# The y sums of a selective scan move into the side work's PSUM bank, and the side work is grouped anew

## The chip, the cores and the metric

The kernel runs on one core of a Trainium2 chip. The metric is the time of one execution on the device in microseconds; before the change the median of three runs is 2876.79 us (2875.39 to 2877.91). All data are float32.

## The reference, cut to what matters

One layer for x of shape [2, 1024, 512]: a gated state-space scan with a residual and a layer norm, then a gated feed-forward block with a residual and a layer norm.

```python
xn = x * rsqrt(mean(x * x) + 1e-6) * norm_w
xn = xn * sigmoid((xn @ select_proj_w.T + select_proj_b) * select_gate)
delta, B_ssm, C_ssm = split(xn @ x_proj_w.T)            # 128 columns each
delta = softplus(delta @ dt_proj_w.T + dt_proj_b)       # [.., 512]
A = -exp(A_log)                                         # [512, 128]
def step(h, inp):                                       # once for each token
    dt, bt, ct, xt = inp
    h = exp(dt[:, :, None] * A) * h + (dt * xt)[:, :, None] * bt[:, None, :]
    y = einsum('bdn,bn->bd', h, ct)
    return h, y
x = layernorm(x + (y + x * D_param) @ out_proj_w.T)
x = layernorm(x + (silu(x @ w_gate.T) * (x @ w_up.T)) @ w_down.T)   # hidden 2048
```

The state h has 512 x 128 values for each batch entry.

## The kernel before

**The scan.** The 2048 tokens are cut into 64 states of S = 32 tokens. The 128 partitions hold the n of the state. A state has two halves, and a half holds 256 of the 512 d's; it is worked in eight steps (r = 0 to 7), each with 32 d's of 32 tokens. So there are 64 x 2 x 8 = 1024 steps k, and the loop over k writes the order of every engine's instructions out by hand.

A step has these instructions, in this order. TensorE makes a group of four matmuls: for b = 0 and 1, `bu` (u times B, L692) for this step, and `a` (A times dt, `decay_mm`, L404) for the next step. ScalarE takes the exponential of each `a` into SBUF (`decay_exp`, L411). VectorE adds what the state before carries over to the first column of each run of tokens (L705) and runs one scan of 1024 elements (L708), which writes a slice of `hs[h]`. The four matmuls of a group stand in four different row strips of the array and run at the same time. GpSimd makes the operands of the groups (`diag`: `ddt` L375, `du` L385).

**C h.** `y_round(h, b)` (L423) sums C h over the partitions for four tokens of a half: four matmuls in four column strips. Eight rounds make a half. They are put into the steps of the next half by `ROUNDS`: rounds 0 to 2 at r = 1, 3 to 5 at r = 4, 6 and 7 at r = 7. Both halves of a state gather in one PSUM bank, `ps_y`. When a state is done, `y_out` copies the bank (ScalarE, L436) and picks and adds the wanted columns (GpSimd, L437 to L439), at r = 0 of the second half of the next state.

**Side work.** What is not the scan is written as Python generators. `pre` makes a lot of 256 tokens ready (names ss, sel, xp, b, z, uT, t0). `post` ends a tile of 128 tokens (zT transposes, op the output projection, layer norm). `ffn` is the feed-forward block of a tile (x1T transposes; gu: gate and up, eight items of eight parts; d: down, four items of eight parts). A generator yields "P" before it takes the bank for an item of matmuls, "H" between the item's parts, and "E" where another engine goes on. Every item takes the one bank of `ps_m` (`misc`), so an item can start only when the item before has been read out: gu by a ScalarE copy (L547), sel and z by ScalarE activations, d by a VectorE add (L567), op and zT by VectorE adds (L474, L461).

**The planner.** `Work.others()` runs at the start of every step and moves each generator that stands at "E" on by one. `Work.tensor()` issues one part: of the item that holds the bank, or of the first generator that waits for it. `PARTS` gives a step its number of parts: up to 4, 3, 3, 3, 3 at r = 0, 2, 3, 5, 6; parts not used are kept as a credit of up to 6, of which a step takes 4 at most. One part is 0.43 to 0.5 us of TensorE: two matmuls of 128 columns (gu), or one of 256 (d, op, sel, xp). Steps with C h have no parts. A lot must be ready before its first state (`work.finish`). What is left of the side work at the loop's end runs in a tail.

**PSUM.** Eight banks: four for `bu` (two buffers of two), two for `a`, one for y, one for the side work.

Of the kernel before, what the change touches and what calls it, by code (L numbers as in the profile page):

```python
# [9 lines left out]
FP = mybir.dt.float32  # L10
AF = mybir.ActivationFunctionType
# [6 lines left out]
TC = 256  # L18


ROUNDS = ((), (0, 1, 2), (), (), (3, 4, 5), (), (), (6, 7))
PARTS = (4, 0, 3, 3, 0, 3, 3, 0)
RMS_EPS = 1e-6
LN_EPS = 1e-5

# [9 lines left out]
def kernel(  # L35
# [83 lines left out]
    pre_pool = tc.alloc_tile_pool(name="pre", bufs=1)  # L119
    step_pool = tc.alloc_tile_pool(name="step", bufs=2)  # L120
    half_pool = tc.alloc_tile_pool(name="half", bufs=2)
    ps_y = tc.alloc_tile_pool(name="ps_y", bufs=1, space=PSUM)
    ps_m = tc.alloc_tile_pool(name="ps_m", bufs=1, space=PSUM)

    bank_pool = [tc.alloc_tile_pool(name="ps_m0", bufs=6, space=PSUM)]
# [39 lines left out]
    def pre(c):  # L165
# [31 lines left out]
        yield "E"  # L197
        for m in range(NM):
            nc.scalar.activation(xT[:, m, :], xT[:, m, :], AF.Copy, scale=col(V_NORM, m))
        yield "P"  # L200
        ps = misc(f"ss_{c}")
        for k in range(NM):
            nc.tensor.matmul(  # L203
# [9 lines left out]
        for a in (slice(0, 2), slice(2, 4)):  # L213
# [1 line left out]
                xn[:, a, :], xT[:, a, :], rms.unsqueeze(1).to_broadcast([P, 2, n]), ALU.mult  # L215
            )
            yield "E"
        yield "P"


        for m in range(NM):
            ps = misc(f"sel_{c}_{m}")
            yield from matmuls(ps, sel_w, m, xn)
            nc.scalar.activation(
                u[:, m, :], ps[:, 0:n], AF.Relu,
                bias=neg[:, 1, m : m + 1], scale=neg[:, 0, m : m + 1],
            )
            nc.scalar.activation(
                dt[:, m, :], ps[:, 0:n], AF.Abs, bias=gate_b[:, m : m + 1], scale=col(V_GATE, m)
            )  # L230
            yield "P" if m + 1 < NM else "E"
        yield from softplus(dt, u)
        nc.scalar.activation(dt, dt, AF.Exp, scale=-1.0)
        yield "E"
        for a in (slice(0, 2), slice(2, 4)):
            nc.gpsimd.tensor_tensor(xn[:, a, :], xn[:, a, :], dt[:, a, :], ALU.mult)
            yield "E"
        yield "P"


        for g, dst in ((0, low), (2, c_sb)):
            ps = misc(f"xp_{c}_{g}")
            yield from matmuls(ps, xp_w, g, xn)
            nc.scalar.copy(dst, ps[:, 0:n])
            yield "P"

        ps = misc(f"b_{c}")
        for j in range(n_j):
# [8 lines left out]
        for st in range(n_s):  # L257
# [2 lines left out]
                ub_d[t0 // S + st, :, :, 1, :].rearrange("g t n -> t g n"),  # L260
                rows.unsqueeze(1).to_broadcast([S, 4, N]),
            )
        yield "P"

        for a in range(0, NM, 2):
            ps = misc(f"z_{c}_{a}")
            for m in (a, a + 1):
                nc.tensor.matmul(  # L268
                    ps[:, ts(m - a, n)], dt_w[:, ts(m, P)], low, start=True, stop=True
                )  # L270
                yield "H" if m == a else "E"
            for m in (a, a + 1):
                z = ps[:, ts(m - a, n)]
                nc.scalar.activation(u[:, m, :], z, AF.Relu, bias=col(V_DTB, m))
                nc.scalar.activation(dt[:, m, :], z, AF.Abs, bias=col(V_DTB, m))
            yield "P" if a == 0 else "E"
        yield from softplus(dt, u)
        for a in (slice(0, 2), slice(2, 4)):
            nc.gpsimd.tensor_tensor(u[:, a, :], dt[:, a, :], xn[:, a, :], ALU.mult)
            yield "E"  # L280

        for j in range(n_j):
            yield "P"
            ps = misc(f"uT_{c}_{j}")
            for m in range(NM):
                nc.tensor.transpose(ps[:, ts(m, P)], u[:, m, ts(j, P)], ident)
                if m == 1:
                    yield "H"
            yield "E"
            t = pre_pool.tile([P, D], FP, tag="row", name=f"uT_{c}_{j}")  # L290
            nc.scalar.copy(
                t.rearrange("p (g m c) -> p m g c", g=4, m=NM),
                ps.rearrange("p (m g c) -> p m g c", m=NM, g=4),
            )
            for st in range(4):
                nc.sync.dma_start(
                    ub_d[t0 // S + 4 * j + st, :, :, 0, :].rearrange("g t q -> t g q"),
                    t[ts(st, S), :].rearrange("t (g q) -> t g q", g=4),
                )
            if c == 0:  # L300
                load(0)
                diag(0, 0)
                diag(0, 1)
        yield "P"
        ps = misc(f"t0_{c}")
        for m in range(NM):
            nc.tensor.matmul(
# [40 lines left out]
    def carry_a(st):  # L348

        if st % NSB == 0:  # L350
            return
        cd = carried[st]
        nc.gpsimd.tensor_tensor(cd, a_n, cd, ALU.mult)
        nc.scalar.activation(cd, cd, AF.Exp, scale=-1.0)

    def carry_h(st, i):

# [57 lines left out]
    def y_round(h, b):  # L415


        st, i = divmod(h, 2)
        if i == 0 and b == 0:
            ys[st] = ps_y.tile([P, 512], FP, tag="y", name=f"y_{st}")  # L420
        at = 28 + 28 * b
        for m in range(NM):
            nc.tensor.matmul(  # L423
                ys[st][ts(m, 32), ts(i, 256)], cz[st % 3][:, at : at + 32],
                hs[h][:, ts(m, 64), ts(b, 4)],
                start=(i == 0 and b == 0), stop=(i == 1 and b == 7),
                skip_group_check=True,
            )

    def y_out(st):  # L430

        tt, s = divmod(st, 4)
        if s == 0:
            yrs[tt] = post_pool.tile([P, 4, P], FP, tag="yr", name=f"yr_{tt}")
        yc = post_pool.tile([P, P, 4], FP, tag="yc", name=f"yc_{st}")
        nc.scalar.copy(yc, ys.pop(st).rearrange("p (q t) -> p q t", t=4))  # L436
        nc.gpsimd.tensor_tensor(yc, yc, pick.unsqueeze(1).to_broadcast([P, P, 4]), ALU.mult)  # L437
        nc.gpsimd.tensor_tensor(yc[:, :, 0:2], yc[:, :, 0:2], yc[:, :, 2:4], ALU.add)
        nc.gpsimd.tensor_tensor(yrs[tt][:, s, :], yc[:, :, 0], yc[:, :, 1], ALU.add)  # L439
        if s == 3:  # L440
            work.add(post(tt), front=True)

    yrs = {}
# [1 line left out]
    def post(tt):  # L445
# [4 lines left out]
        yield "E"  # L450
        nc.gpsimd.tensor_tensor(zT, zT, dq.unsqueeze(2).to_broadcast([P, NM, P]), ALU.mult)
        yield "E"
        yield "P"
        ps = misc(f"zT_{tt}")
        for s in range(4):
            nc.tensor.transpose(ps[:, ts(s, P)], yrs[tt][:, s, :], ident)
# [6 lines left out]
        )  # L463
        x1 = post_pool.tile([P, D], FP, tag="x1", name=f"x1_{tt}", bufs=4)
        nc.sync.dma_start(x1, xf[tt])
        yield "P"
        ps = misc(f"op_{tt}")
        for half in (slice(0, 256), slice(256, 512)):
            for k in range(NM):
# [20 lines left out]
    def ffn(tt, row):  # L490
# [22 lines left out]
            yield "E"  # L513
        fetch(4)
        x1T = ffn_pool.tile([P, NM, P], FP, tag="x1T", name=f"x1T_{tt}")
        yield "P"
        ps = misc(f"x1T_{tt}")
        for m in range(NM):
            nc.tensor.transpose(ps[:, ts(m, P)], row[:, ts(m, P)], ident)
# [5 lines left out]
        for what in order:  # L525
            part = int(what[1])
            if what[0] == "g":
# [2 lines left out]

                for f in range(0, NH, 2):
                    fetch(at + 4)
                    yield "P"
                    ps = misc(f"gu_{tt}_{part}_{f}")
                    for b in range(2):
                        w = pieces[at + b].rearrange("p (a k h) -> p a k h", a=2, k=NM)
# [17 lines left out]
                yield "E"  # L554
            for half in range(2):
                fetch(at + 4)
                yield "P"
                ps = misc(f"d_{tt}_{part}_{half}")
                for f in range(NH):
                    w = pieces[at + f // 4].rearrange("p (f d) -> p f d", f=4)  # L560
                    nc.tensor.matmul(  # L561
                        ps[:, 0:HD], hid[:, f, :], w[:, f % 4, :],
                        start=(f == 0), stop=(f == NH - 1),
                    )
                    yield "H" if f + 1 < NH else "E"
                part_of = row[:, ts(half, HD)]
                nc.vector.tensor_tensor(part_of, part_of, ps[:, 0:HD], ALU.add)  # L567
                at += 2
# [38 lines left out]
    class Work:  # L607


        def __init__(self):  # L610
            self.gens, self.holder = [], None

        def add(self, gen, front=False):
            item = [gen, next(gen)]
# [13 lines left out]
                        self.holder = None  # L628
                    self.step(item)

        def tensor(self):

            if self.holder is not None:
                if self.holder[1] != "H":
                    return False
                self.step(self.holder)
                return True
            for item in self.gens:
                if item[1] == "P":
                    self.holder = item  # L640
                    self.step(item)
                    return True
            return False

        def finish(self, item):
            while item in self.gens:
# [13 lines left out]
    bank_pool.pop().release()  # L660
    bank_pool.append(ps_m)
    ps_bu = tc.alloc_tile_pool(name="ps_bu", bufs=2, space=PSUM)
    ps_a = tc.alloc_tile_pool(name="ps_a", bufs=2, space=PSUM)
    for b in range(2):
        decay_exp(0, b, decay_mm(0, b))

    pres, begun, credit = {}, set(), 0
    for k in range(NG):
        h, m, pair = place(k)
        st, i = divmod(h, 2)  # L670
        r = k % 8
        work.others()
        if r == 0:
            hs[h] = half_pool.tile([P, 256, S], FP, tag="h", name=f"h_{h}")

            if i == 1 and st:
                y_out(st - 1)
            if i == 0:
                c = lot_of[st]
                if c + 1 < NC and c not in begun:  # L680
                    begun.add(c)
                    pres[c + 1] = work.add(pre(c + 1), front=True)
                if st + 1 < NS:
                    if lot_of[st + 1] > c:
                        work.finish(pres[c + 1])
                    load(st + 1)
# [24 lines left out]
            bu.rearrange("p q t -> p (q t)"),  # L711
            0.0, ALU.mult, ALU.add,
        )
        if h:
            for b in ROUNDS[r]:
                y_round(h - 1, b)
        credit = min(credit + PARTS[r], 6)
        for _ in range(min(credit, 4) if PARTS[r] else 0):
            if not work.tensor():
                break  # L720
            credit -= 1

        j, r4 = divmod(k, 4)
        if r4 == 3:
# [7 lines left out]
                carry_h(st + 1, 0)  # L732
        if r == 5 and i == 0 and st + 1 < NS:
            carry_a(st + 1)
    for j in range(8):
        y_round(2 * NS - 1, j)
    y_out(NS - 1)
    ps_a.release()
    ps_bu.release()
    bank_pool[0] = tc.alloc_tile_pool(name="ps_m2", bufs=6, space=PSUM)  # L740
# [4 lines left out]
        work.others()  # L745
        work.tensor()

    for pool in (bank_pool[0], ps_m, ps_y, hid_pool[0], ffn_pool, post_pool, main):
        pool.release()


# [65 lines left out]
```

## Time and profile before

| | |
|---|---|
| median of 3 runs | 2876.79 us |
| the profiled execution | 2875.05 us, span 2873.2 us |
| mean granted TensorE clock | 0.985 |
| TensorE, VectorE busy | 2751.4 us (96%), 2532.2 us (88%) |
| GpSimd, ScalarE busy | 1783.0 us (62%), 1561.8 us (54%) |
| scans, L708 | 1024, 2287 ns each |
| exponentials, L411 | 2048, 585 ns each |
| DMA | 258.66 MB, mean 90 GB/s |

In the groups, a line gives the code line, engine, operation, tiles, shapes and count, then the busy time and the mean of one, then the idle time of the engine ahead of it and who ended it. An fp32 matmul leaves two records, so "x16" of gu is eight matmuls. The time from the first `bu` record of a step to that of the next is called a step's length here; the time from it to the first record of the run behind the group is 1.07 us where nothing waits. Busy time alone says little: the two busiest engines take turns in waiting for each other.

### The profile page before, as it was taken

The page shows a single profiled execution, that of the slowest core. Times are in us where ns is not written, and L with a number is a line of the kernel's source. Part 1 is how long each engine was busy: PE and PEld are TensorE (multiplying, and loading weights), DVE is VectorE, ACT ScalarE, POOL GpSimd, SP SyncE. Part 2 cuts the span into 40 slices and gives each one's busy share as a digit, 9 for nine tenths or more (in the row PEclk, how much of TensorE's full clock was granted, in tenths as well). Part 3 has the DMA queues.
Part 4 walks back from the last instruction along what each step waited for, and adds up shares of the span by engine and source line. Part 5 has one row for each costly group of instructions (what it writes and reads, how often), then busy time and mean ns, then how long its engine had stood idle before and what let it go on. Part 6 is the DMA issues. An engine that isn't in the chain of part 4 may idle for free.

```text
span 2873.2 us, 57382 instructions
## 1 busy us (share of the span) xinstructions
PE 2751.4 (96%) x22728; PEld 1496.3 (52%) x22728; DVE 2532.2 (88%) x2176; ACT 1561.8 (54%) x3105; POOL 1783.0 (62%) x2016
## 2 busy tenths in 40 slices
PE   7879899999999999999999999999999999999998
PEld 4324455555555555455555555555555555555558
DVE  3999799899998999999999999999999999999970
ACT  4545555555565556645555555555556555555543
POOL 4556665666666666666567667566665666666643
PEclk6999999999999999999999999999999999999999
DMA  2011221324213231222312233122321322333236
GB/s 74 16 30 65 78 87 61 105 66 133 85 53 112 89 107 62 82 98 89 111 51 88 97 103 109 56 84 92 114 96 51 115 96 91 114 101 100 98 112 230
DMA packets 112379, 258.66 MB, mean 90 GB/s; under 512 B 11568, under 2 KB 49456, under 8 KB 112112
## 3 DMA queue, kind: packets, MB, share of 16 engines
q1 hardware_dynamic: 112112, 254.99, 27.4%
q8 instruction: 181, 2.97, 0.4%
q14 instruction: 86, 0.70, 0.1%
HBM read 242.23 MB, written 12.71 MB: 89 GB/s over the span
## 4 chain that ended last, share of the span: by engine, by line
PE 75%; DVE 18%; issue 3%; ACT 2%; POOL 1%; DMA 0%; SPq 0%; DVEq 0%; POOLq 0%; ACTq 0%
PE bu L692 27%; PE gu L539 17%; DVE h L708 16%; PE y L423 13%; PE d L561 6%; PE a L404 5%; PE sel L186 2%; PE op L470 1%; PE xp L186 1%; DVE bu L705 1%; ACT a_sb L411 1%; PE b L250 1%; PE ss L203 0%; PE z L268 0%; DMA ub_d<-uT 0%
## 5 line engine op out<-in xcount | busy, mean ns | idle before, releaser
L708 DVE TENSOR_TENSOR_SCAN h<-a_sb,bu 128x1024 f32<-128x1024 f32 x1024 | 2341.2, 2287 | 160.7 <-PE bu L692 46.3
L411 ACT ACTIVATE a_sb<-a 128x496 f32<-128x496 f32 x2048 | 1089.0, 585 | 1078.5 <-PE a L404 957.1
L404 PE MATMUL a<-ddt,a_t 32*128 32x512 f32 x4096 | 1253.9, 647 | 3.0 <-ACT t L314 2.8
L692 PE MATMUL bu<-du,ub 32*128 32x512 f32 x4096 | 1210.5, 647 | 47.9 <-DVE h L708 27.3
L375 POOL TENSOR_TENSOR ddt<-dt,hot 128x512 f32<-128x512 f32 x512 | 532.6, 1048 | 310.2 <-PE a L404 310.2
L539 PEld LDWEIGHTS gu<-x1T,w 128*128 128x128 f32 x4096 | 482.2, 192 | 230.9 <-issue 181.3
L385 POOL TENSOR_TENSOR du<-ub,hot 128x512 f32<-128x512 f32 x512 | 535.0, 1049 | 48.9 <-PE a L404 44.9
L539 PE MATMUL gu<-x1T,w 128*128 128x128 f32 x4096 | 537.1, 283 | 11.7 <-DVE x L474 4.0
L692 PEld LDWEIGHTS bu<-du,ub 32*128 32x128 f32 x4096 | 342.9, 185 | 376.9 <-issue 206.8
L423 PE MATMUL y<-h,cz 128*32 128x256 f32 x8192 | 527.3, 386 | 1.3 <-DVE h L708 1.3
L423 PEld LDWEIGHTS y<-h,cz 128*32 128x32 f32 x8192 | 228.2, 110 | 407.8 <-issue 296.4
L404 PEld LDWEIGHTS a<-ddt,a_t 32*128 32x128 f32 x4096 | 379.4, 185 | 31.3 <-ACT a_sb L411 19.9
L579 POOL TENSOR_SCALAR gu<-gu 128x256 f32<-128x256 f32 x128 | 108.3, 846 | 309.6 <-ACT gu L547 309.3
L705 DVE TENSOR_TENSOR bu<-bu,cd 128x32 f32<-128x32 f32 x992 | 185.6, 187 | 98.2 <-PE a L404 92.0
L561 PE MATMUL d<-w,hid 128*128 128x256 f32 x1024 | 256.7, 393 | 12.6 <-ACT t L314 4.4
L561 PEld LDWEIGHTS d<-w,hid 128*128 128x128 f32 x1024 | 183.9, 190 | 131.7 <-issue 86.1
L437 POOL TENSOR_TENSOR yc<-yc,pick 128x512 f32<-128x512 f32 x64 | 66.5, 1039 | 151.1 <-ACT yc L436 151.0
L362 POOL TENSOR_TENSOR cd<-cd,h 128x256 f32<-128x256 f32 x124 | 106.4, 858 | 45.5 <-DVE h L708 45.5
L587 POOL TENSOR_TENSOR hid<-gu,e 128x256 f32<-128x256 f32 x128 | 93.0, 727 | 62.1 <-ACT e L585 60.2
L547 ACT COPY gu<-gu 128x512 f32<-128x512 f32 x128 | 75.1, 587 | 63.2 <-PE gu L539 63.1
L580 POOL TENSOR_TENSOR gu<-gu 128x256 f32<-128x256 f32 x128 | 94.2, 736 | 10.7
L567 DVE TENSOR_TENSOR x<-x,d 128x256 f32<-128x256 f32 x64 | 25.6, 399 | 72.3 <-PE d L561 72.3
(86 smaller groups left out, 1272.1 us busy)
## 6 DMA issues: line engine op xcount, KB each, us to landing
w<-in_wgu_s_dram SPq DMA_DIRECT2D x256, 512.0 KB, 3.6
w<-in_wd_s_dram SPq DMA_DIRECT2D x128, 512.0 KB, 3.6
cd<-dt_d SPq DMA_DIRECT2D x62, 256.0 KB, 3.9
ub<-ub_d SPq DMA_DIRECT2D x64, 128.0 KB, 2.0
ub_d<-bt SPq DMA_DIRECT2D x64, 64.0 KB, 1.8
ub_d<-uT SPq DMA_DIRECT2D x64, 64.0 KB, 1.8
zT<-in_x_q_dram SPq DMA_DIRECT2D x16, 256.0 KB, 4.1
x<-in_x_dram SPq DMA_DIRECT2D x16, 256.0 KB, 3.8
```

The lines of the kernel that those rows point to most:

```text
L362: nc.gpsimd.tensor_tensor(cd, cd, last, ALU.mult)
L375: nc.gpsimd.tensor_tensor(ddts[j][:, m, :, :], made[lot_of[st]][0][:, a + m, toks(st)].unsqueeze(1).to_broadcast([P, 16, S]), hot[:, ts(i, ...
L385: nc.gpsimd.tensor_tensor(dus[j][:, m, :, :], uv[:, a + m, :].unsqueeze(2).to_broadcast([P, 16, S]), hot.unsqueeze(1).to_broadcast([P, 16, ...
L404: nc.tensor.matmul(ps, a_t[ts(g, 32), m, :], ddts[k // 4][ts(g, 32), m % 2, :, :], start=True, stop=True,)
L411: nc.scalar.activation(a_sb[:, k % 3, ts(b, 16), 1:], ps[:, :, 1:], AF.Exp, scale=-1.0)
L423: nc.tensor.matmul(ys[st][ts(m, 32), ts(i, 256)], cz[st % 3][:, at : at + 32], hs[h][:, ts(m, 64), ts(b, 4)], start=(i == 0 and b == 0), s ...
L539: nc.tensor.matmul(ps[:, ts(2 * a + b, P)], w[:, a, k, :], x1T[:, k, :], start=(k == 0), stop=(k == NM - 1),)
L561: nc.tensor.matmul(ps[:, 0:HD], hid[:, f, :], w[:, f % 4, :], start=(f == 0), stop=(f == NH - 1),)
L579: nc.gpsimd.tensor_scalar_max(g, g, -80.0)
L692: nc.tensor.matmul(bu[:, ts(b, 16), :], prepared[st][ts(g, 32), 1, :], dus[k // 4][ts(g, 32), m % 2, :, :], start=True, stop=True,)
L705: nc.vector.tensor_tensor(first, first, left[:, at : at + 2, i, :], ALU.add)
L708: nc.vector.tensor_tensor_scan(hs[h][:, ts(r, 32), :].rearrange("p q t -> p (q t)"), a_sb[:, k % 3, :, :].rearrange("p q t -> p (q t)"), b ...
```

## The change

- y of one half has its own tile now, taken from the side work's bank (`misc`) and not from a bank for both halves. All eight rounds are issued at r = 2 and r = 3 of the next half, four each. `y_out` runs once for each half, at r = 4, on 256 columns.
- The free bank goes to `a`: `ps_a` has three buffers.
- `PARTS` has six groups: 2 and 3 parts at r = 0 and 1, 3 each at r = 4 to 7. The credit is gone. A generator yields its item's number of parts where it yielded "P", and an item starts only where `ROOM` allows its length. Before the rounds at r = 2, `work.idle()` issues all that is left of an item that holds the bank.
- The exponential of the carried decay (`carry_exp`) is issued at r = 7, not at r = 5.

```diff
-ROUNDS = ((), (0, 1, 2), (), (), (3, 4, 5), (), (), (6, 7))
-PARTS = (4, 0, 3, 3, 0, 3, 3, 0)
+ROUNDS = ((), (), (0, 1, 2, 3), (4, 5, 6, 7), (), (), (), ())
+PARTS = (2, 3, 0, 0, 3, 3, 3, 3)
+
+ROOM = (8, 4, 0, 0, 24, 20, 16, 12)
...
         cd = carried[st]
         nc.gpsimd.tensor_tensor(cd, a_n, cd, ALU.mult)
-        nc.scalar.activation(cd, cd, AF.Exp, scale=-1.0)
+
+    def carry_exp(st):
+        if st % NSB:
+            nc.scalar.activation(carried[st], carried[st], AF.Exp, scale=-1.0)
...
-        st, i = divmod(h, 2)
-        if i == 0 and b == 0:
-            ys[st] = ps_y.tile([P, 512], FP, tag="y", name=f"y_{st}")
+        if b == 0:
+            ys[h] = misc(f"y_{h}")
...
-        yc = post_pool.tile([P, P, 4], FP, tag="yc", name=f"yc_{st}")
-        nc.scalar.copy(yc, ys.pop(st).rearrange("p (q t) -> p q t", t=4))
+        yc = post_pool.tile([P, 64, 4], FP, tag="yc", name=f"yc_{h}", bufs=2)
+        nc.scalar.copy(yc, ys.pop(h)[:, 0:256].rearrange("p (q t) -> p q t", t=4))
...
-        def tensor(self):
+        def tensor(self, room=64):
...
             for item in self.gens:
-                if item[1] == "P":
-                    self.holder = item
+                if item[1] != "E" and item[1] <= room:
+                    self.holder, self.left = item, item[1] - 1
                     self.step(item)
                     return True
             return False
+
+        def idle(self):
+
+            while self.holder is not None:
+                self.others()
+                if self.holder is not None:
+                    self.tensor()
...
-    ps_a = tc.alloc_tile_pool(name="ps_a", bufs=2, space=PSUM)
+    ps_a = tc.alloc_tile_pool(name="ps_a", bufs=3, space=PSUM)
...
+        if r == 4 and h:
+            y_out(h - 1)
...
-        if h:
+        if ROUNDS[r] and h:
+            if r == 2:
+                work.idle()
             for b in ROUNDS[r]:
                 y_round(h - 1, b)
-        credit = min(credit + PARTS[r], 6)
-        for _ in range(min(credit, 4) if PARTS[r] else 0):
-            if not work.tensor():
-                break
-            credit -= 1
+        done = 0
+        while done < PARTS[r] and work.tensor(ROOM[r] - done):
+            done += 1
...
+        if r == 7 and i == 0 and st + 1 < NS:
+            carry_exp(st + 1)
```

More of the change, by code (lines that the diff above doesn't have):

```diff
@@ L121 @@
     half_pool = tc.alloc_tile_pool(name="half", bufs=2)
-    ps_y = tc.alloc_tile_pool(name="ps_y", bufs=1, space=PSUM)
     ps_m = tc.alloc_tile_pool(name="ps_m", bufs=1, space=PSUM)
@@ L199, in pre @@
             nc.scalar.activation(xT[:, m, :], xT[:, m, :], AF.Copy, scale=col(V_NORM, m))
-        yield "P"
+        yield NM
         ps = misc(f"ss_{c}")
@@ L217, in pre @@
             yield "E"
-        yield "P"
+        yield NM
         for m in range(NM):
@@ L230, in pre @@
             )
-            yield "P" if m + 1 < NM else "E"
+            yield NM if m + 1 < NM else "E"
         yield from softplus(dt, u)
@@ L237, in pre @@
             yield "E"
-        yield "P"
+        yield NM
         for g, dst in ((0, low), (2, c_sb)):
@@ L244, in pre @@
             nc.scalar.copy(dst, ps[:, 0:n])
-            yield "P"
+            yield NM if g == 0 else n_j
         ps = misc(f"b_{c}")
@@ L262, in pre @@
             )
-        yield "P"
+        yield 2
         for a in range(0, NM, 2):
@@ L275, in pre @@
                 nc.scalar.activation(dt[:, m, :], z, AF.Abs, bias=col(V_DTB, m))
-            yield "P" if a == 0 else "E"
+            yield 2 if a == 0 else "E"
         yield from softplus(dt, u)
@@ L282, in pre @@
         for j in range(n_j):
-            yield "P"
+            yield 2
             ps = misc(f"uT_{c}_{j}")
@@ L303, in pre @@
                 diag(0, 1)
-        yield "P"
+        yield 1
         ps = misc(f"t0_{c}")
@@ L423, in y_round, with y_out @@
             nc.tensor.matmul(
-                ys[st][ts(m, 32), ts(i, 256)], cz[st % 3][:, at : at + 32],
+                ys[h][ts(m, 32), 0:256], cz[h // 2 % 3][:, at : at + 32],
                 hs[h][:, ts(m, 64), ts(b, 4)],
-                start=(i == 0 and b == 0), stop=(i == 1 and b == 7),
+                start=(b == 0), stop=(b == 7),
                 skip_group_check=True,
             )
-    def y_out(st):
+    def y_out(h):
+        st, i = divmod(h, 2)
         tt, s = divmod(st, 4)
-        if s == 0:
+        if s == 0 and i == 0:
             yrs[tt] = post_pool.tile([P, 4, P], FP, tag="yr", name=f"yr_{tt}")
-        yc = post_pool.tile([P, P, 4], FP, tag="yc", name=f"yc_{st}")
-        nc.scalar.copy(yc, ys.pop(st).rearrange("p (q t) -> p q t", t=4))
-        nc.gpsimd.tensor_tensor(yc, yc, pick.unsqueeze(1).to_broadcast([P, P, 4]), ALU.mult)
+        yc = post_pool.tile([P, 64, 4], FP, tag="yc", name=f"yc_{h}", bufs=2)
+        nc.scalar.copy(yc, ys.pop(h)[:, 0:256].rearrange("p (q t) -> p q t", t=4))
+        nc.gpsimd.tensor_tensor(yc, yc, pick.unsqueeze(1).to_broadcast([P, 64, 4]), ALU.mult)
         nc.gpsimd.tensor_tensor(yc[:, :, 0:2], yc[:, :, 0:2], yc[:, :, 2:4], ALU.add)
-        nc.gpsimd.tensor_tensor(yrs[tt][:, s, :], yc[:, :, 0], yc[:, :, 1], ALU.add)
-        if s == 3:
+        nc.gpsimd.tensor_tensor(yrs[tt][:, s, ts(i, 64)], yc[:, :, 0], yc[:, :, 1], ALU.add)
+        if s == 3 and i == 1:
             work.add(post(tt), front=True)
@@ L452, in post @@
         yield "E"
-        yield "P"
+        yield 2
         ps = misc(f"zT_{tt}")
@@ L465, in post @@
         nc.sync.dma_start(x1, xf[tt])
-        yield "P"
+        yield 2 * NM
         ps = misc(f"op_{tt}")
@@ L515, in ffn @@
         x1T = ffn_pool.tile([P, NM, P], FP, tag="x1T", name=f"x1T_{tt}")
-        yield "P"
+        yield 2
         ps = misc(f"x1T_{tt}")
@@ L532, in ffn @@
                     fetch(at + 4)
-                    yield "P"
+                    yield 2 * NM
                     ps = misc(f"gu_{tt}_{part}_{f}")
@@ L556, in ffn @@
                 fetch(at + 4)
-                yield "P"
+                yield NH
                 ps = misc(f"d_{tt}_{part}_{half}")
@@ L610, in __init__ @@
         def __init__(self):
-            self.gens, self.holder = [], None
+            self.gens, self.holder, self.left = [], None, 0
         def add(self, gen, front=False):
@@ L635, in tensor @@
                     return False
+                self.left -= 1
                 self.step(self.holder)
@@ L662 @@
     ps_bu = tc.alloc_tile_pool(name="ps_bu", bufs=2, space=PSUM)
-    ps_a = tc.alloc_tile_pool(name="ps_a", bufs=2, space=PSUM)
+    ps_a = tc.alloc_tile_pool(name="ps_a", bufs=3, space=PSUM)
     for b in range(2):
         decay_exp(0, b, decay_mm(0, b))
-    pres, begun, credit = {}, set(), 0
+    pres, begun = {}, set()
     for k in range(NG):
@@ L672 @@
         work.others()
+        if r == 4 and h:
+            y_out(h - 1)
         if r == 0:
             hs[h] = half_pool.tile([P, 256, S], FP, tag="h", name=f"h_{h}")
-            if i == 1 and st:
-                y_out(st - 1)
             if i == 0:
@@ L734 @@
             carry_a(st + 1)
+        if r == 7 and i == 0 and st + 1 < NS:
+            carry_exp(st + 1)
+    work.idle()
     for j in range(8):
         y_round(2 * NS - 1, j)
-    y_out(NS - 1)
+    y_out(2 * NS - 1)
     ps_a.release()
@@ L746 @@
         work.tensor()
-    for pool in (bank_pool[0], ps_m, ps_y, hid_pool[0], ffn_pool, post_pool, main):
+    for pool in (bank_pool[0], ps_m, hid_pool[0], ffn_pool, post_pool, main):
         pool.release()
```

## The prediction

> **What bounds the kernel now.** I read the page first: shares of the engines, then the chain that ended last, then the groups.
>
> ```profile
> PE 2751.4 (96%) x22728; PEld 1496.3 (52%) x22728; DVE 2532.2 (88%) x2176; ACT 1561.8 (54%) x3105; POOL 1783.0 (62%) x2016
> ...
> PE 75%; DVE 18%; issue 3%; ACT 2%; POOL 1%; DMA 0%; SPq 0%; DVEq 0%; POOLq 0%; ACTq 0%
> ...
> L708 DVE TENSOR_TENSOR_SCAN h<-a_sb,bu 128x1024 f32<-128x1024 f32 x1024 | 2341.2, 2287 | 160.7 <-PE bu L692 46.3
> ```
>
> TensorE and VectorE share the bound. A step k is one group of four matmuls (bu and a, L692 and L404) and then one run (C h, or side work), and one scan. VectorE needs 2.29 for the scan and 0.19 for L705: 2.48 us a step, 19.84 a half. For TensorE I read run lengths from the chain in a quiet stretch (start, us, what):
>
> ```profile
> 1000.57 1.43 PE y L423 x24
> ...
> 1024.14 1.98 PE gu L539 x16
> ...
> 1030.24 1.00 PE y L423 x16
> ...
> 1038.10 1.54 PE gu L539 x12
> ...
> 1045.82 1.09 PE gu L539 x8
> ```
>
> A run costs 0.43 to 0.44 per round or part (8 records of y, 4 of gu, 2 of d, sel, xp or op) and 0.1 to 0.2 for its start: gu 0.64, 1.09, 1.53, 1.98 for 1 to 4 parts; d and its like 0.63, 1.06, 1.49, 1.93; four y rounds, by that slope, 1.87. The group before it takes 1.07. So the old step lasts 3.05 with four parts, 2.50 and 2.07 with three and two rounds. On these lengths alone TensorE needs 19.9 to 20.1 a half; the trace shows about 21.4. The difference is waits, and two of them carry this forecast. The first, in the order of time:
>
> ```profile
> 1240.12 0.69 PE L692 MATMUL bu<-du,ub 32*128 32x512 f32 x1
> ...
> 1241.33 1.06 ACT L411 ACTIVATE a_sb<-a 128x496 f32<-128x496 f32 x2 [1.55 <-PE a L404]
> ...
> 1241.84 0.69 PE L692 MATMUL bu<-du,ub 32*128 32x512 f32 x1
> 1242.05 0.66 PE L404 MATMUL a<-ddt,a_t 32*128 32x512 f32 x1
> ...
> 1242.44 0.71 PE L404 MATMUL a<-ddt,a_t 32*128 32x512 f32 x2
> ...
> 1243.49 1.07 PE L423 MATMUL y<-h,cz 128*32 128x256 f32 x16
> ```
>
> A step of one part (1.72) brings the next group before ScalarE has emptied the two A dt banks: exponentials until 1242.39, second a at 1242.44. The run then starts 1.65 after its group's start and not 1.07. In general it starts no earlier than 3.37 after the start of the group before.
>
> The second is a hand-over of the side bank. A d item ends with two parts, VectorE adds it to the row (L567), and the next item waits:
>
> ```profile
> 2178.41 0.69 PE L692 MATMUL bu<-du,ub 32*128 32x512 f32 x1
> ...
> 2179.48 1.13 PE L561 MATMUL d<-w,hid 128*128 128x256 f32 x4
> ...
> 2179.95 2.29 DVE L708 TENSOR_TENSOR_SCAN h<-a_sb,bu 128x1024 f32<-128x1024 f32 x1
> 2180.54 0.69 PE L692 MATMUL bu<-du,ub 32*128 32x512 f32 x1
> ...
> 2182.16 0.39 DVE L567 TENSOR_TENSOR x<-x,d 128x256 f32<-128x256 f32 x1
> ...
> 2182.61 1.99 PE L561 MATMUL d<-w,hid 128*128 128x256 f32 x8 [0.77 <-DVE x L567]
> ```
>
> The add stands behind the whole scan; the run starts 2.07 after its group, 1.00 late. Such pairs are rare before: the y runs at r = 1, 4, 7, in their own bank, lie between most items.
>
> **Part 1, the third A dt bank.** The second a then waits for the first exponential of the group before, 0.53 earlier: the limit of 3.37 becomes 2.84. A cycle of 16 halves (one lot, two tiles) has before: 16 steps with two rounds (2.07; each makes the next run 0.23 late), about 8 of one part (1.71; 0.59), 6 of zT, x1T or uT (1.66; 0.64) and 2.5 empty ones (1.07; 1.23): 3.7 + 4.7 + 3.8 + 3.1 = 15.3 us. With three banks about 0.6 is left. Removed: 14.7 a cycle.
>
> **Part 2, the new order.** Following the planner's rules of the changed code, the loop falls into a pattern that repeats every 16 halves (r = 0 to 7; "+" marks parts that `idle` forces in ahead of y at r = 2):
>
> ```
> d2 d3 y4 y4 ss3 ss1 gu3 gu3    | gu2 zT2 y4 y4 op3 op3 op2 sel3
> sel1 sel3 +sel1 y4 y4 sel3 sel1 sel3 sel1 | gu2 gu3 +gu3 y4 y4 xp3 xp1 xp3 xp1
> b2 z2 y4 y4 z2 gu3 gu3 gu2     | gu2 gu3 +gu3 y4 y4 uT2 uT2 t1 d3
> d2 d3 y4 y4 d3 d3 d2 x1T2      | gu2 gu3 +gu3 y4 y4 gu3 gu3 gu2 gu3
> gu2 gu3 y4 y4 gu3 gu3 gu2 zT2  | op2 op3 +op3 y4 y4 d3 d3 d2 d3
> d2 d3 y4 y4 gu3 gu3 gu2 gu3    | gu2 gu3 y4 y4 gu3 gu3 gu2 gu3
> gu2 gu3 y4 y4 d3 d3 d2 d3      | d2 d3 y4 y4 x1T2 gu3 gu3 gu2
> gu2 gu3 +gu3 y4 y4 gu3 gu3 gu2 gu3 | gu2 gu3 y4 y4 d3 d3 d2 d3
> ```
>
> TensorE's lengths: 128 groups 137.0, 32 y runs 59.8, gu 32 x 1.53 + 16 x 1.09 = 66.4, d 16 x 1.49 + 8 x 1.06 = 32.3, op 8.1, sel, xp and ss 14.8, the rest 8.7: 327.1 a cycle, for 255 parts. Before: 317.7 to 321.0, for 240 to 247.
>
> **Part 3, y in the side bank.** Now y waits for the item ahead of it, and the new order puts hand-overs side by side. Waits per cycle:
> - d2 then a side run (r = 6 to 7): four at 1.00, the row above: 4.0.
> - d3 then y (r = 1 to 2): four. The add ends where it did in the row, 4.20 after d's group; the step is 2.56 and the group 1.07, so 0.57; the short step ahead lets the scan fall 0.35 further behind: 0.92 each, 3.7.
> - zT then op, and zT then y: 1.74 each, the mean of the trace's six zT-op pairs (run 2.81 after its group): 3.5. op then sel: 1.39 (such pairs start at 2.46).
> - Forced parts: gu, four times its copy (0.59, and 0.13 of signals), 2.9; sel, two copies behind two exponentials, 1.8; op, whose add stands behind this step's own scan: 1.9 + 2.29 + 0.66 + 0.1 - 2.56 = 2.4 at most, 2.0 taken.
> - Three sel pairs at 0.33 and two after z at 0.80, their rows: 2.6.
>
> Sum 21.9, where before I count 4.4. Behind a waiting y or side matmul stand the next group's bu and a in TensorE's queue, and for those wait the next scan and exponentials; a scan runs at most some 1.05 us (lead of 2.6 against 1.55 at least) on work done ahead, so waits of 1 to 2 us beside runs of four rounds (step 2.94 against 2.48) reach VectorE. VectorE's own pace adds some 2 us in both. A rule speaks against this part: the Trainium skill, "PSUM — Partial Sum Buffer", section on bank collisions, says that a TensorE write and a read by another engine may not meet in one bank. By the rule alone a y run waits for 0.40 of add, which the next group (1.07) covers: no charge outside the forced parts. By the row it is 1.00, because of VectorE's queue. I take the row.
>
> **Small edits.** y_out: one ScalarE copy of 585 ns a state becomes two of about 373 (the 128x256 c_sb copies), at r = 4 under the group; GpSimd's 2.07 us become 2.1 to 3.2 (half the length, or the 736 ns of a 128x256 product in place of half of 1039), at 62% busy. Uncovered, they would be late for du; those waits are 19 us now. The exponential of cd (631 ns) moves from r = 5 to 7: ScalarE idled 15.3 us for it, off the chain; it is needed at r = 1 of the second half. The scans of a half no longer share r = 7 with its reader's last rounds, which held nothing up. No DMA is added; fetches move with their items.
>
> **Clock.** After two of the six zT-op waits the granted clock fell by half and op took 3.64 in place of 2.0:
>
> ```profile
> 1113.00:1116.00 3.00, 3.00 (x11) 1.90 (x14) 1.95 (x1) 0.00 (x0) 1.46 (x3) 0.50 0.00 0
> ```
>
> The skill's "TensorE: Matmul & The Clock Gate", Part 1, asks for a whole idle window of about 3.4 us before the gate closes; these waits are 1.7 to 1.9. By the rule: nothing. By the rows, about 18 added waits of 1.4 to 2 us, a third of them 1.6 each: 10 us. I take 5.
>
> **Sum.** Cycle after: 327.1 + 21.9 + 0.6 + 2 = 351.6. Before, the five cycles that start at halves 32 to 96 last 340 to 346, mean 342.2. The loss of 9.4 over 119 halves (7.4 cycles; start-up left out) is +69. Side work left for the tail falls from 164 to 129 parts; the tail's rows price one:
>
> ```profile
> 2822.80 30.48 PE gu L539 x256
> ```
>
> 64 parts in 30.48, so 35 parts give back 16. Clock +5. Total +58: 2875.05 (profiled execution; span 2873.2) becomes 2933, and the median of 2876.79 about **2935**.
>
> **Rivals.**
> - **The hand-overs are hidden, and the third bank decides: faster.** One mechanism: wherever VectorE is late with an add, VectorE sets the pace and TensorE's wait is free. For it: several old pairs stand where scans lag 2.3 to 3.4 us behind the group, not 1.55. Against: after a wait and four rounds the next scan starts 3.9 after the end of the last but one, and VectorE's own work in between is 2.9. Then 12.6 of the 21.9 go: 3.2 x 7.4 = -24, tail -16, so 2837. It decides the sign where under some 40% of those 12.6 are paid (-24 + 93 x 0.4 - 16 is about nothing).
> - **The waits are dearer.** The scan lags more after empty-ish steps, d3-y costs up to 1.8, d2 hand-overs 1.15, and the clock drops often: 26 a cycle, clock +10: 2970.
> - **It cancels:** the third bank pays for the hand-overs within 6 us: 2877.
>
> **Chances.** Likeliest case (2895 to 2955) 0.63, dearer 0.21, hidden 0.11, cancelled 0.05. A measurement of this kernel tells 0.2% (6 us) from no change: faster 0.11, same 0.04, slower 0.85. The range of 2885 to 2990 leaves out the hidden and cancelled cases and the top of the dear one.
>
> **What would show it.** Right: a rows no longer late after short steps; the waits of y at r = 2 on DVE x L567, ACT gu L547 and DVE zT L461, new; d waits on L567 several times 17 us; a tail some 16 us shorter; about 21.9 to 22.1 a half. Wrong: y starts 1.07 after its group after d items, or VectorE stays busy through such steps.

## The result and the profile after

The changed kernel takes 3009.48 us (3003.42 to 3012.13), against 2876.09 (four runs) for the kernel before: 1.0462 times as long, 95% interval 1.0444 to 1.048. Slower was forecast, at 2935 us; the loss is 133 us and not 58. The profiled execution is the fastest of its four (3003.42 us), 6 us under the median.

The page of the changed kernel, the rows that answer to those shown before:

```profile
PE 2712.9 (90%) x22728; PEld 1443.5 (48%) x22728; DVE 2546.1 (85%) x2176; ACT 1574.3 (52%) x3169; POOL 1819.1 (61%) x2208
...
PE 70%; DVE 17%; ACT 6%; issue 4%; POOL 1%; DMA 1%; SPq 1%; DVEq 0%; ACTq 0%; POOLq 0%
...
L720 DVE TENSOR_TENSOR_SCAN h<-a_sb,bu 128x1024 f32<-128x1024 f32 x1024 | 2340.4, 2287 | 153.6 <-PE bu L704 40.7
...
L426 PE MATMUL y<-h,cz 128*32 128x256 f32 x8192 | 504.6, 387 | 91.9 <-DVE x L571 26.6
```

Both bounding engines are idle for longer than before (TensorE 90% of the span, VectorE 85%), and ScalarE now has 6% of the chain, where it had 2%. TensorE is idle for 91.9 us ahead of the y matmuls; before, it was 1.3 us:

```profile
L423 PE MATMUL y<-h,cz 128*32 128x256 f32 x8192 | 527.3, 386 | 1.3 <-DVE h L708 1.3
```

Where the 128 us between the two profiled spans (2873.2 and 3001.5) lie, read from the starts of the groups: the first 256 steps take 17.8 more (749.8 against 732.0), the five cycles from step 256 to 896 take 364.1 each against 342.1 (5 x 22.0 = 109.8), the last 128 steps to the end of the last scan 17.3 more; the tail behind it gives back 16.7 (71.3 against 88.0). The tail was forecast at -16 and a cycle at +9.4.

For a cycle I took, in each step, how much later than 1.07 after its group a run starts (or later than the end of the run ahead of it, for y behind forced parts), and how much later than the run's end the next group starts, and added that up by pairs. A run's end is here the time at which the next group starts where nothing waits, some 0.07 before the end of its last record. Us per cycle, mean of the five; "total" is the cycle less the bare lengths, so it also holds runs that took longer than usual:

```
pair                     forecast   before   after
total                      24.5      22.0     37.0
d, then y                   3.7       0.8      3.7
d, then d or x1T            4.0       0.6      4.7
zT, then op or y            3.5       1.8      3.8
op, then sel                1.4       0.3      1.2
forced gu, then y           2.9       -        4.5
forced op, then y           2.0       -        1.9
forced sel, then y          1.8       -        1.5
sel or z, then another      2.6       0.8      3.6
uT, then t0                  -        0.0      1.5
t0, then d                   -        0.4      2.2
x1T, then gu                 -        0.9      2.1
```

In each of the five cycles the runs are those of the forecast's pattern, step by step, and undisturbed they have its lengths, so the bare lengths are 327.1 us as forecast. The hand-overs are there too, most of them near their price. This is d, then y, in the changed kernel, in the order of time:

```profile
1775.59 0.69 PE L704 MATMUL bu<-du,ub 32*128 32x512 f32 x1
...
1776.66 1.56 PE L565 MATMUL d<-w,hid 128*128 128x256 f32 x6
...
1777.55 2.29 DVE L720 TENSOR_TENSOR_SCAN h<-a_sb,bu 128x1024 f32<-128x1024 f32 x1
1778.15 0.69 PE L704 MATMUL bu<-du,ub 32*128 32x512 f32 x1
...
1779.76 0.40 DVE L571 TENSOR_TENSOR x<-x,d 128x256 f32<-128x256 f32 x1
...
1780.21 1.93 PE L426 MATMUL y<-h,cz 128*32 128x256 f32 x32 [0.92 <-DVE x L571]
```

y starts 2.06 after its group, 0.99 late (0.92 forecast), because the add stands behind the scan. What the forecast did not have is in three other places.

**The row of uT and t0.** `pre` copies each transposed block into one SBUF buffer (tag "row") and sends it to DRAM. Here two uT items and t0 follow each other at r = 4, 5, 6:

```profile
1605.31 7.29 SPq L297 DMA_DIRECT2D ub_d<-uT  x8
...
1608.47 0.59 ACT L292 COPY uT<-uT 128x512 f32<-128x512 f32 x1 [2.01 <-DMA ub_d<-uT]
1608.96 1.07 ACT L415 ACTIVATE a_sb<-a 128x496 f32<-128x496 f32 x2
...
1609.11 1.05 PE L308 MATMUL t<-ident,dt 128*8 128x128 f32 x8 [1.45 <-ACT uT L292]
...
1614.03 0.58 ACT L315 COPY t<-t 8x512 f32<-8x512 f32 x1 [4.01 <-DMA ub_d<-uT]
1614.52 1.03 ACT L415 ACTIVATE a_sb<-a 128x496 f32<-128x496 f32 x2
...
1614.66 2.93 PE L565 MATMUL d<-w,hid 128*128 128x256 f32 x6 [3.43 <-ACT t L315]
```

ScalarE stands still for 2.0 and 4.0 us, until the DMAs of the row before have gone; the exponentials and the bank wait with it. The d run behind t0 then takes 2.93 us in place of 1.56, to which the last section comes back. In the kernel before, a y run stood just ahead of t0 in four of the five cycles.

**A norm behind y's sums.** `y_out` moved to r = 4. There GpSimd waits for ScalarE's copy of y, and the small operation of a layer norm (off) stands behind y's three sums and one ddt; behind it stand ScalarE's x and x1T and TensorE's gu:

```profile
1785.60 0.61 POOL L441 TENSOR_TENSOR yc<-yc,pick 128x256 f32<-128x256 f32 x1 [5.00 <-ACT yc L440]
...
1788.17 0.26 POOL L489 TENSOR_SCALAR off_f<-mv_f,rstd_f 128x1 f32<-128x1 f32 x1
...
1788.47 0.81 ACT L490 ACTIVATE x<-x,off_f,rstd_f 128x512 f32<-128x512 f32 x1 [1.21 <-POOL off_f L489]
...
1789.19 0.56 ACT L527 COPY x1T<-x1T 128x512 f32<-128x512 f32 x1
...
1789.81 1.80 PE L543 MATMUL gu<-x1T,w 128*128 128x128 f32 x12 [1.84 <-ACT x1T L527]
```

**Forced parts behind `pre`.** `idle()` calls `others()` again and again in one step, which moves every generator. So in one of the four forced gu items of a cycle an exponential of `pre` comes ahead of the gu copy, and waits for GpSimd. Between the records, y starts 2.19 us after this gu, and 0.68 after each of the other three:

```profile
1549.99 1.60 PE L543 MATMUL gu<-x1T,w 128*128 128x128 f32 x12
...
1552.21 1.06 ACT L234 ACTIVATE dt<-dt 128x1024 f32<-128x1024 f32 x1 [1.03 <-POOL dt L325]
1553.17 0.57 ACT L551 COPY gu<-gu 128x512 f32<-128x512 f32 x1
...
1553.79 1.93 PE L426 MATMUL y<-h,cz 128*32 128x256 f32 x32 [2.19 <-ACT gu L551]
```

### The profile page after: what moved, and what is told of

Read it like the earlier page. It is cut to its first block, busy times and chain, and to the rows that moved or that the text cites. A ratio compares the mean times of both kernels' runs of the same rounds, so it can differ in the third digit from the quotient of the medians.

```text
span 3001.5 us, 57964 instructions
## 1 busy us (share of the span) xinstructions
PE 2712.9 (90%) x22728; PEld 1443.5 (48%) x22728; DVE 2546.1 (85%) x2176; ACT 1574.3 (52%) x3169; POOL 1819.1 (61%) x2208
## 4 chain that ended last, share of the span: by engine, by line
PE 70%; DVE 17%; ACT 6%; issue 4%; POOL 1%; DMA 1%; SPq 1%; DVEq 0%; ACTq 0%; POOLq 0%
PE bu L704 27%; PE gu L543 16%; PE y L426 16%; DVE h L720 14%; PE d L565 5%; ACT a_sb L415 2%; PE a L408 2%; PE sel L187 1%; PE op L474 1%; DVE bu L717 1%; DMA ub_d<-uT 1%; DVE x L571 1%; PE xp L187 1%; SPq L297 1%; PE ss L204 1%
## 5 line engine op out<-in xcount | busy, mean ns | idle before, releaser
L704 PE MATMUL bu<-du,ub 32*128 32x512 f32 x4096 | 1196.5, 656 | 55.0 <-DVE bu L717 45.6
L408 PE MATMUL a<-ddt,a_t 32*128 32x512 f32 x4096 | 1207.2, 657 | 2.8 <-ACT t L315 2.8
L426 PE MATMUL y<-h,cz 128*32 128x256 f32 x8192 | 504.6, 387 | 91.9 <-DVE x L571 26.6
L543 PE MATMUL gu<-x1T,w 128*128 128x128 f32 x4096 | 555.5, 285 | 26.3 <-ACT x1T L527 16.9
L389 POOL TENSOR_TENSOR du<-ub,hot 128x512 f32<-128x512 f32 x512 | 533.7, 1048 | 16.7 <-PE a L408 12.4
L704 PEld LDWEIGHTS bu<-du,ub 32*128 32x128 f32 x4096 | 325.7, 187 | 369.9 <-issue 218.6
L426 PEld LDWEIGHTS y<-h,cz 128*32 128x32 f32 x8192 | 242.3, 111 | 409.8 <-issue 116.8
L408 PEld LDWEIGHTS a<-ddt,a_t 32*128 32x128 f32 x4096 | 333.0, 187 | 5.7 <-issue 3.3
L565 PE MATMUL d<-w,hid 128*128 128x256 f32 x1024 | 276.1, 406 | 35.8 <-DVE x L571 19.5
L441 POOL TENSOR_TENSOR yc<-yc,pick 128x256 f32<-128x256 f32 x128 | 78.4, 612 | 371.6 <-ACT yc L440 367.9
L187 PE MATMUL sel<-xT,sel_w 128*128 128x256 f32 (+1 forms) x288 | 74.4, 387 | 16.4 <-DVE x L478 6.9
```

What stands on the lines that cost most here:

```text
L187: nc.tensor.matmul(ps[:, 0:n], w[:, k, ts(m, P)], rhs[:, k, :], start=(k == 0), stop=(k == NM - 1),)
L389: nc.gpsimd.tensor_tensor(dus[j][:, m, :, :], uv[:, a + m, :].unsqueeze(2).to_broadcast([P, 16, S]), hot.unsqueeze(1).to_broadcast([P, 16, ...
L408: nc.tensor.matmul(ps, a_t[ts(g, 32), m, :], ddts[k // 4][ts(g, 32), m % 2, :, :], start=True, stop=True,)
L426: nc.tensor.matmul(ys[h][ts(m, 32), 0:256], cz[h // 2 % 3][:, at : at + 32], hs[h][:, ts(m, 64), ts(b, 4)], start=(b == 0), stop=(b == 7), ...
L543: nc.tensor.matmul(ps[:, ts(2 * a + b, P)], w[:, a, k, :], x1T[:, k, :], start=(k == 0), stop=(k == NM - 1),)
L565: nc.tensor.matmul(ps[:, 0:HD], hid[:, f, :], w[:, f % 4, :], start=(f == 0), stop=(f == NH - 1),)
```

## The experiments

The theory is that sharing the bank costs most, because each hand-over waits for another engine's queue, and that what the forecast lacks are the three waits just shown. The rivals: the new order loses by itself; the waits take each other's place, so that mending one gains nothing. Times are medians; the kernel before was 2874 to 2876 us in every session, and gains are counted from the changed kernel's 3009.48 us (3003 to 3012) of the first.

**y in its own bank, two A dt banks.** The order stays.

```diff
+    ps_y = tc.alloc_tile_pool(name="ps_y", bufs=1, space=PSUM)
...
-            ys[h] = misc(f"y_{h}")
+            ys[h] = ps_y.tile([P, 512], FP, tag="y", name=f"y_{h}")
...
-    ps_a = tc.alloc_tile_pool(name="ps_a", bufs=3, space=PSUM)
+    ps_a = tc.alloc_tile_pool(name="ps_a", bufs=2, space=PSUM)
```

> The new order with y in a bank of its own and two A dt banks. If the shared bank is the loss: the waits of y at r = 2 (14.1 us a cycle of 16 halves in the trace of the changed kernel) go, the waits of a after short steps come back (some 10 us a cycle), 2930 to 2960 us. If the new order itself or the queues behind it are the loss, and sharing only shows where time is lost anyway: 2990 or more.

2933.99 us, 1.0203 (1.0181 to 1.0225), in the range expected for the shared bank. y's waits behind d and forced gu are gone (0.0 a cycle), and the waits of a are back at about half of what was expected (runs held at the 3.37 limit: 5.4 a cycle). The order without sharing costs 58 us against the kernel before.

**Two A dt banks only.**

```diff
-    ps_a = tc.alloc_tile_pool(name="ps_a", bufs=3, space=PSUM)
+    ps_a = tc.alloc_tile_pool(name="ps_a", bufs=2, space=PSUM)
```

> The changed kernel with two A dt banks; one bank lies unused. If the third bank earns what the forecast's limits of 3.37 and 2.84 us say, in an order with fewer short steps: 20 to 40 us slower than the changed kernel, 3030 to 3050. If it earns nothing there: 3009.

3023.43 us, 1.0509 (1.0494 to 1.0525): 14 slower than the changed kernel, less than expected. In the list of waits the line of the exponentials is the sign of it; the changed kernel first, then this one (us in total, times, longest):

```profile
PEld a L408 <- ACT a_sb L415: 2.2, 5, 0.5
```

```profile
PEld a L408 <- ACT a_sb L415: 16.7, 81, 0.6
```

With the two runs the change falls into three, taken in this order: the new order +58 (2876 to 2934), sharing the bank +89 (to 3023), the third bank -14 (to 3009). Sharing shows in the cycle: with two A dt banks it is 352.2 us with y in its own bank and 364.8 with the shared one. The third bank hardly does. Runs held at the 3.37 limit fall from 5.3 us a cycle to 0.1, but the cycle only from 364.8 to 364.1, because later next groups (0.5 to 2.2) and longer runs (2.1 to 2.6) make up for most of it. Of the 20.2 us between the two profiled spans (3021.7 and 3001.5) 19.8 lie in the first 256 steps. There the granted clock is low in both (0.92 and 0.94 over the first 750 us), and how much of this is the bank is not shown.

**Three row buffers.**

```diff
-            t = pre_pool.tile([P, D], FP, tag="row", name=f"uT_{c}_{j}")
+            t = pre_pool.tile([P, D], FP, tag="row", name=f"uT_{c}_{j}", bufs=3)
...
-        t = pre_pool.tile([P, D], FP, tag="row", name=f"t0_{c}")
+        t = pre_pool.tile([P, D], FP, tag="row", name=f"t0_{c}", bufs=3)
```

> The changed kernel with three SBUF buffers in place of one for the rows that pre sends out (uT twice, then t0). If ScalarE's copies that wait for these DMAs hold up TensorE (uT to t0 1.5 and t0 to d 2.2 us a cycle in the trace): 25 to 35 us faster than the changed kernel, 2975 to 2985. If that wait only takes the place of another: within 6 us of 3009.

2971.1 us: 38 faster than the changed kernel. The copies follow their matmuls at once:

```profile
1590.32 3.72 SPq L297 DMA_DIRECT2D ub_d<-uT  x8
...
1591.36 0.59 ACT L292 COPY uT<-uT 128x512 f32<-128x512 f32 x1
1592.61 0.76 PEld L308 LDWEIGHTS t<-ident,dt 128*8 128x8 f32 x8 [0.76 <-ACT uT L292]
1592.61 1.05 PE L308 MATMUL t<-ident,dt 128*8 128x128 f32 x8
1593.69 0.57 ACT L315 COPY t<-t 8x512 f32<-8x512 f32 x1
```

uT then t0 and t0 then d are 0.0 a cycle. The gain is larger than the 3.7 x 7.4 = 27 that these pairs show. The traces have a second part of it: the d run behind t0 takes 2.48 to 2.93 us in all five cycles of the changed kernel, at a granted clock of 0.50 to 0.60. Here it takes its usual 1.56 in all five, at 1.00. That is 5.9 us over the five cycles, beside 18.7 for the pairs; other waits grew a little, and the five cycles together are 21.6 us shorter.

**d read out by ScalarE.**

```diff
-                nc.vector.tensor_tensor(part_of, part_of, ps[:, 0:HD], ALU.add)
+                dp = ffn_pool.tile([P, HD], FP, tag="dp", name=f"dp_{tt}_{part}_{half}")
+                nc.scalar.copy(dp, ps[:, 0:HD])
+                nc.vector.tensor_tensor(part_of, part_of, dp, ALU.add)
```

> The changed kernel with d taken out of the side bank by a ScalarE copy (128x256 into SBUF); VectorE adds from there. If hand-overs of d wait for VectorE's queue: d to y (3.7 us a cycle) and d to the next item (4.7) vanish, some 60 us faster than the changed kernel, 2940 to 2955. If VectorE sets the pace in those steps: no gain, 3005 to 3015.

2975.75 us: 34 faster, about half of what was expected. d then y falls to 0.0 and d then d to 0.3 a cycle, 8.1 less with x1T; but 5.5 less is all that the cycle gains (358.6 against 364.1). Later next groups take back 4.2, most of it waiting for VectorE, and other waits are some 1.6 less. The list of waits, the changed kernel first:

```profile
PE bu L704 <- DVE bu L717: 45.6, 59, 1.4
...
PEld bu L704 <- DVE h L720: 10.0, 14, 2.0
PE bu L704 <- DVE h L720: 6.1, 11, 1.0
```

```profile
PE bu L706 <- DVE bu L719: 54.5, 80, 1.4
...
PEld bu L706 <- DVE h L722: 21.9, 25, 2.0
PE bu L706 <- DVE h L722: 18.3, 26, 2.0
```

This looks like the rival of the forecast that calls such waits free where VectorE sets the pace. But the edit also makes VectorE's part dearer, so it does not settle that. The add now reads both operands from SBUF:

```profile
L573 DVE TENSOR_TENSOR x<-x,dp 128x256 f32<-128x256 f32 x64 | 50.8, 794 | 57.7 <-ACT dp L572 57.7
```

The add out of the bank takes 396 ns. In the five cycles the eight adds of a cycle take 6.7 us in place of 3.2, 3.5 more, against the 4.2 that came back. How much of d's waits VectorE's own pace had covered is not shown.

**GpSimd's y sums at r = 5.** ScalarE's copy stays at r = 4.

```diff
...
+        if r == 5 and h:
+            y_sum(h - 1, yc)
...
```

> The changed kernel with GpSimd's three operations of y_out at the end of r = 5 and not at r = 4 (ScalarE's copy stays). If the norm's small GpSimd operation (off) stands behind them, and with it ScalarE's x1T copy and TensorE's first gu (2.1 us a cycle): 5 to 15 us faster than the changed kernel, 2994 to 3004. If the x1T copy is late for another reason: within 4 us of 3009.

2987.52 us: 22 faster, more than expected. The norm's operation now comes ahead of the sums:

```profile
1780.49 0.26 POOL L494 TENSOR_SCALAR off_f<-mv_f,rstd_f 128x1 f32<-128x1 f32 x1 [3.32 <-ACT rstd_f L613]
...
1781.72 0.61 POOL L448 TENSOR_TENSOR yc<-yc,pick 128x256 f32<-128x256 f32 x1
```

x1T then gu falls from 2.1 to 0.8 a cycle, so the queue was the cause of that wait. Another 0.9 a cycle is the d run behind t0: in four of five cycles it takes 1.56 us again, though it starts as late as before (1.8 to 1.9). So the granted clock differs there (1.00 over these four runs, 0.50 to 0.60 over the five of the changed kernel), and not the wait; why it stayed up is not shown.

**idle() for the holder alone.**

```diff
             while self.holder is not None:
-                self.others()
-                if self.holder is not None:
-                    self.tensor()
+                item = self.holder
+                if item[1] == "E":
+                    self.holder = None
+                self.step(item)
```

> The changed kernel with an idle() that moves only the item that holds the bank, and no other generator. If the forced gu copies wait behind pre's ScalarE work, which the repeated others() puts ahead of them in one step (4.5 us a cycle in place of the 2.9 of the forecast): 8 to 15 us faster than the changed kernel, 2994 to 3001. If the wait is that of the copy alone: within 4 us of 3009.

2992.53 us: 17 faster, a little more than expected. The forced gu that stood behind `pre` now costs y 0.68 in place of 2.19, in each of the five cycles, like the others: the cause is shown. The edit also shifts the pattern, though: another forced gu became a forced d (1.6), and t0 then d (2.2) became t0 then x1T (1.3). So 1.5 a cycle, some 11 us, is what this wait itself is worth by the trace, and the 17 us hold other things too.

**All four mends**, and **all four with y in its own bank** and two A dt banks.

> The changed kernel with all four mends: three row buffers, d read out by ScalarE, GpSimd's y sums at r = 5, idle() for the holder alone. If the four waits are separate losses, their gains add up (38 and 34 measured, some 20 more expected): 2905 to 2925. If one wait takes the place of another: 2940 or more.

> All four mends, y in its own bank, two A dt banks: only the order of the changed kernel is left against the kernel before. If the order as such costs nothing, and its loss of 58 us (2934 with its own bank) is the row buffer, d's hand-overs and the two queues: 2845 to 2875. If the new order loses by its grouping itself (parts that no longer fill the steps, one more run start): 2890 to 2920.

2911.63 us, 1.0138 (1.0113 to 1.0162), and 2871.64 us, 0.9992 (0.9986 to 0.9999). Both lie in the ranges for separate losses: the four gains are 111 one by one and 98 together. With all of them, sharing still costs 40 us net of the third bank, and the order costs nothing against the kernel before as it stands.

**The kernel before, mended.** The row buffers alone, then with d read out by ScalarE.

> The kernel before with three row buffers. Its trace shows the same waits behind the row's DMAs, spread by the y runs that lie between (y to t 0.8, uT to uT 0.6, t to d 0.4, after uT 0.8 us a cycle). If they cost what they show: 10 to 20 us faster than before, 2855 to 2866. If the y runs hide them: 2870 or more.

> The same with d read out by ScalarE too. Hand-overs of d that wait are few in the old order (d to y 0.8, d to d 0.5, d to gu 0.5, d to zT 0.3 us a cycle) and ScalarE's copies add 0.37 each ahead of exponentials with two A dt banks: 0 to 10 us faster than with the rows alone. If ScalarE's queue is the dearer one in this order: slower than with the rows alone.

2857.11 us, 0.9942 (0.9929 to 0.9956), and 2852.41 us, 0.9924 (0.9912 to 0.9937). Both are faster than the kernel before and than the changed one, and both are in the ranges expected. The second step is 5 us; the two intervals overlap, but all five runs with it (2850.2 to 2853.6) lie below all five without it (2856.5 to 2858.5). With the same two mends, and the two that belong to the new order, the new order in its own banks is 19 us slower than this. So mended against mended the order still costs something.

That forced parts be left out altogether, by a tighter `ROOM`, was not tried; the side work would fall behind further, and whether its buffers could hold that is not shown. A third A dt bank in the old order was not tried either, since all eight banks are in use there.

## Why the prediction was wrong

- **What bounds it, the run lengths and the pattern** were right. The 16 halves repeat as written, with 255 parts and 327.1 us of bare lengths.
- **Part 1, the third bank:** the mechanism was right, its size was not. In the trace before, the runs that start at the limit (3.30 to 3.44 after the group before) are late by 8.6 us a cycle, not 15.3. All waits before still total 22.0 a cycle, against 21.7 in the forecast's sums (15.3 + 4.4 + 2), because other waits were larger; that agreement is luck. It did not make the miss, because the forecast adds up the new cycle by itself and sets it against the measured 342.2.
- **Part 3, the shared bank, is the step that failed:** its list of waits was too short. A cycle has 37.0 us of waits where the forecast has 24.5. The pairs that it priced came to 24.9 against 21.9. So the row was the right guide, and the rule set against it was not: the wait is that of the reader's queue. Of the 12.5 that are missing, 5.8 are uT, t0 and x1T, which the list leaves out. Another 1.6 are the forced gu, priced at the bare copy, and 1.4 the other priced pairs. Runs that took longer than usual make 2.6 (0.9 before), and the remaining waits, of next groups and small ones, are 3.7 against the 2.6 allowed for. What was missed first of all is in-order queues that the moved steps passed: ScalarE behind the row's DMAs, GpSimd behind y's sums, ScalarE behind `pre`. The runs that mend the three gain 38, 22 and 17 us. That these 77 are near the 75 that the forecast was short is partly luck, since they also hold the granted clock and waits that the edits shifted.
- **Small edits:** the forecast has GpSimd's sums covered, and du late if they are not. What was late, and cost, was the norm's off. TensorE's waits for du grew too (19.6 to 34.9 us in all), but they stay when the sums move to r = 5 (36.9), so the sums are not their cause.
- **Tail:** -16 was forecast and -16.7 found. The mechanism was right: the parts left for it fall from 164 to 132, where 129 were forecast.
- **Clock and start-up:** the mean granted clock is 0.973 against 0.985. In the cycles the longer runs alone cost 1.7 us more than before (2.6 against 0.9). Over 7.4 cycles that is some 12 us by estimate, where the forecast took 5. The first 256 steps lose 17.8 us, where the forecast's rate over their last 24 halves gives 14; how much of that is the clock is open.
- **Rivals:** "hidden" did not come true; whether it holds for some of d's waits is not shown (8.1 a cycle removed, 5.5 gained, with a dearer add). "Dearer" named the right direction, and its clock term of 10 us is near the estimate of 12, but d then y kept its price (3.7), and what was dear was not in its list.

## What to carry to other kernels

A bank that two kinds of work share is handed over at the speed of the reader's queue, not of the read (here a 0.40 us add behind a 2.29 us scan): look up what stands ahead of the read on its engine, at the place where it will be. When an order is packed closer, go through every single-buffered tile of the moved items, the SBUF rows that DMAs drain as well as the banks, and ask what used to lie between. A loop that "lets everybody go on" to free one resource puts strangers' work ahead of what it waits for.

## What was not expected of the hardware

The granted clock can fall after waits of TensorE that are short. The changed kernel, around the t0 item (the column after the engines' busy times is the clock):

```profile
1606.00:1613.00 7.00, 3.35 (x25) 1.31 (x24) 6.69 (x7) 2.01 (x4) 5.61 (x7) 1.00 0.30 68
1613.00:1618.00 5.00, 3.34 (x10) 2.32 (x14) 0.92 (x1) 1.51 (x3) 1.86 (x2) 0.56 0.45 83
```

After 3.4 us of waiting the next run has 0.56, and six d records take 2.93 in place of 1.56. After the 1.84 us ahead of gu at 1789.81 the clock is 0.68 (1790 to 1793). After the 2.19 us ahead of y at 1553.79, 32 y records take their usual 1.93. The Trainium skill, "TensorE: Matmul & The Clock Gate", Part 1, ties the drop to an idle window of about 3.4 us; here it came after 1.84 and stayed away after 2.19, so the length of one wait doesn't decide it. The d run behind t0 says the same: where it starts 1.8 to 1.9 late, it takes 2.5 to 2.8 us in the changed kernel (three of five cycles), and 1.56 in four of five with GpSimd's sums at r = 5.
